# Block transposes and moves in place of PE transposes for 16 of 26 context chunks in a cross-attention kernel

## The chip, the core and the metric

The kernel runs on one core of a Trainium2 chip, and the metric is the time of one execution on the device in microseconds. The core has a matrix engine (PE, which multiplies and accumulates into PSUM), a vector engine (DVE), a scalar engine (ACT), GpSimd (POOL) and a sync engine (SP), which here only issues transfers. ACT issues transfers too. PE's weight loads are listed apart as PEld. All data are 32-bit floats.

## The reference, cut to what matters

The computation is a cross-attention layer followed by a small recurrence. Only the first lines bear on the change: the context `ctx_1024` (3202 keys of 512 features) is layer-normalised and projected to keys and values for 8 heads of 64.

```python
x = _layernorm(builder_state, g1, beta1)          # 4096 x 512 queries
base_n = _layernorm(base_state, g1, beta1)        # 3202 x 512 context
x = residual + _mha(x, base_n, W_qkv, b_qkv, W_o, b_o)
# inside _mha, per head:
#   k = base_n @ Wk.T + bk ; v = base_n @ Wv.T + bv
#   attn = softmax(q k^T / 8) ; out = attn @ v
xn = _layernorm(x, g2, beta2)
U = (xn @ W_in.T + b_in) @ Bmat
# s_t = silu(s_{t-1} @ A.T) + u_t, over all t
x = residual + states @ Cmat + mod
```

Softmax and the weighted sum over keys do not depend on the order of the keys, as long as keys and values have the same order.

## The kernel before, in words

The program has two large stages. The first, the preparation, turns the context into keys and values and stores them in device memory; it takes the first 216 us. The second, attention, goes through 64 units (blocks of 512 queries by pairs of heads, in halves), with a planner that orders its pieces by costs and due times; the recurrence and the output rows run beside it. The change touches the preparation alone. Its instructions are in a fixed order, written out by hand (`manual_schedule`): each engine and each transfer queue runs its own instructions in the order of the program text.

The context is worked in 26 chunks of 128 keys (the last has 2), in groups of `GC = 4`. For chunk c:

- `load_chunk` (L544) loads it from device memory into `cx`, on SP's queue, five chunks ahead in program order.
- `norm_chunk` makes its statistics on DVE (L259, L261), three small operations on POOL (L268, L270, L272) and the normalised rows `xh` on ACT (L280). The loop does this for chunk c+3.
- `turn_chunk`, for chunk c+2, transposes `xh` in four 128x128 blocks on PE (L296, tile `tp_c`) and copies the result from PSUM into the group's tile `ct`, on ACT for even chunks and on DVE for odd ones (L575). `ct` holds features on the partitions and keys along the row; two such tiles alternate.
- The values: eight matmul instructions with `ct` as the stationary operand (L623, tile `pv`), a copy to `vs` on ACT (L636) and a store `vd` on SP (L637).
- At the end of a group the keys: for each of the four head pairs (`hp`) eight matmul instructions with `ct` as the moving operand (L656, tile `pk`), the bias on ACT into `ks` (L664) and two stores `kd` on SP (L669). `pv` and `pk` have two PSUM tiles each.

Between these, a generator called `side` is advanced by one step at a time (`next(work)`, once per chunk and once or twice per head pair). It holds work on the weights and constants (loads on ACT's queue of `win`, `cb`, `rowb`, `modb`, `wp_t`, `a_t`, `wo`; small products such as `pw`, `pt`, `pb`; the sum `sums` over `cb`, L509, and its product `pm`, L515) and then the first queries: four tiles are normalised, transposed on PE (`tp_x`, L296) and copied, and three head pairs of queries are made (`pq`, L325).

The functions `flip` and `move` are already used in attention, for query rows and output rows: `flip` transposes 32x32 blocks of one chunk by one DVE instruction (L1057) into half of the columns of a pair of chunks, and `move` carries one band of 32 partitions of that pair to its place in the transposed tile by four transfers within SBUF of 32 KB each (L1069). Four moves serve one pair; each gives 64 columns, in which 32 come from one chunk and 32 from the other.

Of the kernel before, what the change touches and what calls it, by code (L numbers as in the profile page):

```python
# [10 lines left out]
F32 = mybir.dt.float32  # L11
# [8 lines left out]
T, S2, H, NH, HD, NS = 4096, 3202, 512, 8, 64, 64  # L20
P = 128
TB = 32
NC = H // P
NCH = 26
CK = 128
NDC = NCH // 2
REST = S2 - (NCH - 1) * CK
GC = 4
# [3 lines left out]
QU = QB // 2  # L32
LAG = 4
FIRST = 3
EPS = 1e-5
L = 16
LT = 4
# [16 lines left out]
def keys(c):  # L54


    return CK if c < NCH - 1 else REST


def blocks(c):  # L60

    return 2 if c < NDC - 1 else 1


def key0(c):
    return c * CK
# [117 lines left out]
def xattn_ssm_kernel(  # L184
# [22 lines left out]
    nc = tc.nc  # L207
# [56 lines left out]
    def factors(mv, n, name, pool=None):  # L264

        pool = pool or ln
        ve = pool.tile([P, 1], F32, tag="ve", name=f"ve_{name}")
        nc.gpsimd.tensor_scalar(ve[:n], mv[:n, 1:2], EPS, None, ALU.add)  # L268
        rstd = pool.tile([P, 1], F32, tag="rstd", name=f"rstd_{name}")
# [71 lines left out]
    def first_queries(x0):  # L341

        xn = first_xn["xn"] = xnp.tile([P, NC, QB], F32, tag="xn", name="xn_0")
        for t in range(NT):
# [10 lines left out]
            yield  # L355
        for hp in range(FIRST):
            pieces = heads(0, hp, xn)
# [34 lines left out]
    wp = prep.enter_context(tc.tile_pool(name="wkv", bufs=1))  # L392
    cin = prep.enter_context(tc.tile_pool(name="cin", bufs=3))
    ctp = prep.enter_context(tc.tile_pool(name="cT", bufs=2))
# [140 lines left out]

    cxs, xhs, cts = {}, {}, {}

    def load_chunk(c):  # L540
        if c < NCH:
# [5 lines left out]
    def norm_chunk(c):  # L547
        if c < NCH:
            xhs[c] = normalize(cxs.pop(c), keys(c), f"c{c}", pool=cin)


    def first_chunk(c):
        xt, name = cxs.pop(c), f"c{c}"
        mv = stats(xt, P, name, cin)
        ve = cin.tile([P, 1], F32, tag="ve", name=f"ve_{name}")
        nc.vector.tensor_scalar(ve, mv[:, 1:2], EPS, None, ALU.add)
        rstd = cin.tile([P, 1], F32, tag="rstd", name=f"rstd_{name}")
# [8 lines left out]
    def turn_chunk(c):  # L566
        if c < NCH:
            g, n = c // GC, keys(c)
            if c % GC == 0:
                cts[g] = ctp.tile([P, NC, GC * CK], F32, tag="ct", name=f"ct_{g}")  # L570
            o = key0(c) - key0(g * GC)
            copy = nc.vector.tensor_copy if c % 2 else nc.scalar.copy
            tp = transposes(kps, "t", xhs.pop(c), n, f"c{c}")
            for cs in (slice(0, 2), slice(2, NC)) if c == 0 else (slice(0, NC),):
                copy(cts[g][:, cs, o : o + n], tp[:, cs])  # L575

    with tc.manual_schedule():
        load_chunk(0)
        nc.scalar.dma_start(g1s, g1)
        fetch_w(2, nc.scalar, slice(0, NC // 2))  # L580
        fetch_w(2, nc.sync, slice(NC // 2, NC))
        load_chunk(1)
        load_chunk(2)
        fetch_w(1, nc.sync)
        load_chunk(3)
        idle = m_tile([P, 512], "idle")
        nc.scalar.copy(bu, neg_half)
        for _ in range(11):
            nc.tensor.matmul(idle[:, :P], a_t, a_t, start=True, stop=True)
        for t, src in ((be1s, beta1), (bqkv, b_qkv), (g2s, g2), (be2s, beta2)):  # L590
            nc.sync.dma_start(t, src)
        for c in range(4, 5):
            load_chunk(c)
        early = [first_chunk(c) for c in range(2)]
        next(early[0])
        next(early[0])
        turn_chunk(0)
        gain(2, wv, 0)
        gain(2, wv, 1)
        next(early[1])  # L600
        gain(2, wv, 2)
        norm_chunk(2)
        gain(2, wv, 3)
        next(early[1])
        work = side()
        first = shift(1)
        loads = [partial(load_k, *steps[k]) for k in range(AHEAD_K - 1)]
        loads += [partial(load_v, *steps[k]) for k in range(AHEAD - 1)]
        for c in range(NCH):
            load_chunk(c + 5)  # L610
            if c >= 2 * AHEAD_K:
                for _ in range(4):
                    if loads:
                        loads.pop(0)()
            norm_chunk(c + 3)
            g, n = c // GC, keys(c)
            ct, o = cts[g], key0(c) - key0(g * GC)
            pv = kps.tile([P, 512], F32, tag="v", name=f"pv_{c}")
            parts = 1 if c < NCH - 1 else 2
            for i in range(NC // parts):  # L620
                for h in range(parts):
                    k = h * NC // parts + i
                    nc.tensor.matmul(  # L623
                        pv[h * HD : h * HD + n, :H],
                        ct[:, k, o : o + n],
                        wv[:, k, :],
                        start=(i == 0),
                        stop=(i == NC // parts - 1),
                        skip_group_check=True,
                    )  # L630
            if c == 0:
                turn_chunk(1)
            turn_chunk(c + 2)
            if c < NCH - 1:
                vs = cin.tile([CK, NC, P], F32, tag="vs", name=f"vs_{c}")
                nc.scalar.copy(vs, pv)  # L636
                nc.sync.dma_start(vd[:, c // 2, :, c % 2, :].rearrange("h p d -> p h d"), vs)  # L637
            else:
                second = wp.tile([n, H], F32, name="second")
                nc.scalar.copy(second, pv[HD : HD + n])  # L640
                nc.vector.tensor_tensor(vx[:n], pv[:n], second, ALU.add)
                nc.sync.dma_start(vx[HD : HD + n], vx[:n])
            if c < GC:
                if c == 1:
                    gain(1, wk)
                for _ in range((0, 0, 1, 2)[c]):
                    next(first)
            else:
                next(work, None)
            if c % GC < GC - 1 and c < NCH - 1:  # L650
                continue
            n_g = o + n
            for hp in range(NC):
                pk = kps.tile([P, 512], F32, tag="k", name=f"pk_{g}_{hp}")
                for i in range(NC):
                    nc.tensor.matmul(  # L656
                        pk[:, :n_g],
                        wk[:, i, hp * P : (hp + 1) * P],
                        ct[:, i, :n_g],
                        start=(i == 0),  # L660
                        stop=(i == NC - 1),
                    )
                ks = cin.tile([P, GC * CK], F32, tag="ks", name=f"ks_{g}_{hp}")
                nc.scalar.activation(  # L664
                    ks[:, :n_g], pk[:, :n_g], AF.Identity, bias=bias[:, NC + hp : NC + hp + 1]
                )
                for b in range(g * GC, c + 1, 2):
                    m, k = blocks(b // 2) * CK, key0(b) - key0(g * GC)
                    nc.sync.dma_start(kd[hp, b // 2, :, :m], ks[:, k : k + m])  # L669
                if g == 0:  # L670
                    nc.gpsimd.tensor_copy(kx[:, hp, REST:], ks[:, : HD - REST])
                elif c == NCH - 1:
                    nc.gpsimd.tensor_copy(kx[:, hp, :REST], ks[:, CK : CK + REST])
                for _ in range(2 if g > 1 else 1):
                    next(work, None)
        left = sum(1 for _ in work)
        assert left == 0, left
# [315 lines left out]
    def queries(plan, Q, d):  # L993
# [55 lines left out]
                    copied.append((*ks[t], "copy"))  # L1049
            d += 2 * QSTEP  # L1050
        head_pieces(plan, Q, range(NC), w, copied, d, QSTEP // 2, [("xn", of_xn)])

    def flip(pair, xh, t):

        nc.vector.transpose(  # L1057
            pair.rearrange("p t h -> p (t h)").rearrange("p (g t r) -> p t g r", t=2, r=TB)[:, t],
            xh.rearrange("p (g r) -> p g r", r=TB),
        )  # L1060

    def move(xn, pair, a):

        n = 2 * TB
        of = pair[a * TB : (a + 1) * TB].rearrange("p t h -> p (t h)").rearrange(
            "p (c b k) -> p b c k", b=P // TB, k=n
        )
        for b in range(P // TB):
            nc.sync.dma_start(xn[b * TB : (b + 1) * TB, :, a * n : (a + 1) * n], of[:, b])  # L1069

    def mixed(of, t):
        return of.rearrange("p (a t r) -> p t a r", t=2, r=TB)[:, t]
# [507 lines left out]
    def unit(plan, i):  # L1580
# [16 lines left out]
        w["shift"] = shifts[:, Q * NC + hp : Q * NC + hp + 1]  # L1597
        q = [("q", Q, hp)] if Q or hp >= FIRST else []
        first = i if half == 0 else index[Q, hp, 0]
# [281 lines left out]
    with tc.manual_schedule():  # L1881
# [5 lines left out]
                xn=1, xh=2, max=2, rd=2, o_=12,  # L1887
            ),
            dict(q=[("heads", 0, hp) for hp in range(FIRST)], xn=["first"]),
        )  # L1890
        head_pieces(plan, 0, range(FIRST, NC), first_xn, [("spread", 0)], -40 * STEP, 0, [("xn", "first")], "o")
        index = {at_: i for i, at_ in enumerate(units)}
# [12 lines left out]
    n = nc.values_load(sv["nbad"][0:1, 0:1], min_val=0, max_val=P * (NCK + P // LT + 3 * len(units)))  # L1905
    with tc.If(n > 0, label="general"):
# [14 lines left out]
        with tc.For_i(0, 2 * P // LT, 1):  # L1921
            sl, th, h = sv["sl"], sv["thl"], sv["hw"][:, : P // LT]
# [71 lines left out]
```

## Time and profile before

| | |
|---|---|
| runs | 1963.19, 1963.2, 1960.02 us; median 1963.19 |
| profiled execution | 1960.71 us, span 1958.9, mean granted clock 0.996 |
| PE busy | 98% of the span |
| DVE, ACT, POOL busy | 74%, 60%, 12% |
| preparation | from 0 to about 216 us |
| context transposes on PE | 104 instructions, the first at 6.1, the last at 192.7 us |
| key stretches (L656) | from 25.7, 56.7, 91.0, 122.8, 152.9, 192.8 and 212.0 us |

In a timeline row the first two numbers are the start and the length in us, then the engine (with q: its instruction queue, as for issues of transfers), the line, the operation, and the output tile with its inputs; brackets hold the idle time of the engine before it and what ended that. In a group row the last numbers are the count, then busy us and mean ns. In a wait row they are the total, the number of times and the longest. In a row on transfers they are the count, the KB of each and the median us from issue to landing.

### The profile page before, as it was taken

The numbers are of one execution on the slowest core, as the hardware profiler recorded it, in microseconds if no ns is written. First come the engines' busy times: TensorE is split into PE (matmuls) and PEld (weight loads), VectorE is DVE, ScalarE is ACT, GpSimd is POOL, SyncE is SP. The second block draws the span as 40 slices with busy tenths as digits, with TensorE's granted clock in tenths as the row PEclk, the third lists the DMA queues.
The fourth block names the chain that finished last, engine by engine and source line by source line (L and its number), as shares of the span: only waits on it lengthen the run. The fifth ranks groups of instructions, "written<-read, shape, count | busy, mean of one in ns | idle before, by whom it ended". The sixth has DMA issues, their size and how long they took to land. (4 is left out here: it accounts for less than half of the span.)

```text
span 1958.9 us, 66935 instructions
## 1 busy us (share of the span) xinstructions
PE 1928.9 (98%) x29092; PEld 1259.3 (64%) x29092; DVE 1459.3 (74%) x1983; ACT 1171.3 (60%) x1632; POOL 225.5 (12%) x374
## 2 busy tenths in 40 slices
PE   9999999999999999999999999999999999999996
PEld 5444577666667666666667666666666666766674
DVE  4321489688878887888868886888778886877876
ACT  2233477566666666666657665666666675665653
POOL 2111000001200120011100120012001100011105
PEclk9999999999999999999999999999999999999998
DMA  6533234123422243223312342224322331544476
GB/s 195 172 102 108 64 85 115 48 86 88 129 79 80 86 114 84 74 83 109 104 47 86 92 121 77 81 87 122 87 82 75 95 96 43 156 134 141 143 207 199
DMA packets 246935, 204.28 MB, mean 104 GB/s; under 512 B 80809, under 2 KB 220073, under 8 KB 246637
## 3 DMA queue, kind: packets, MB, share of 16 engines
q1 hardware_dynamic: 242616, 193.32, 34.1%
q10 hardware_dynamic: 4020, 6.62, 1.1%
q8 instruction: 231, 3.78, 0.8%
q14 instruction: 68, 0.55, 0.1%
HBM read 156.32 MB, written 29.88 MB: 95 GB/s over the span
## 5 line engine op out<-in xcount | busy, mean ns | idle before, releaser
L783 ACT ACTIVATE p<-s,shifts 128x1024 f32<-128x1024 f32 (+1 forms) x832 | 890.1, 1081 | 482.9 <-PE s L706 474.3
L791 DVE TENSOR_TENSOR acc<-p,acc 128x1024 f32<-128x1024 f32 (+1 forms) x704 | 830.5, 1180 | 203.6 <-ACT p L783 169.8
L840 PE MATMUL po<-p,v 64*64 64x256 f32 x12800 | 834.1, 377 | 2.7 <-DVE o L889 2.5
L706 PE MATMUL s<-q,k 64*64 64x256 f32 x12800 | 834.9, 377 | 1.8 <-ACT p L783 1.8
L706 PEld LDWEIGHTS s<-q,k 64*64 64x64 f32 x12800 | 490.4, 133 | 214.2 <-issue 13.3
L840 PEld LDWEIGHTS po<-p,v 64*64 64x64 f32 x12800 | 485.0, 133 | 192.6 <-issue 12.0
L1110 POOL TENSOR_TENSOR xr<-xr,rowb 128x512 f32<-128x512 f32 x30 | 42.7, 1436 | 984.9 <-DMA xr<-in_x_dram 984.9
L912 DVE RECIPROCAL rd<-rd 128x256 f32<-128x256 f32 (+1 forms) x64 | 110.2, 1722 | 13.0 <-ACT rd L907 12.7
L325 PE MATMUL pq<-xn,wq 128*128 128x512 f32 x248 | 110.7, 598 | 0.0
L1116 PE MATMUL pa<-wo,o 128*128 128x512 f32 x240 | 107.0, 599 | 0.0
L623 PE MATMUL pv<-wv,ct 128*128 128x512 f32 (+1 forms) x208 | 92.6, 595 | 0.9 <-DVE wv L406 0.9
L656 PE MATMUL pk<-ct,wk 128*128 128x512 f32 (+1 forms) x224 | 88.9, 550 | 0.0
L575 DVE COPY ct<-tp_c 128x512 f32<-128x512 f32 (+1 forms) x13 | 8.4, 649 | 105.7 <-PE tp_c L296 105.7
L791 DVE TENSOR_TENSOR acc<-p,p 128x1024 f32<-128x1024 f32 x64 | 78.1, 1221 | 10.6 <-ACT p L783 10.6
L325 PEld LDWEIGHTS pq<-xn,wq 128*128 128x128 f32 x248 | 45.7, 190 | 55.5 <-issue 54.3
L1116 PEld LDWEIGHTS pa<-wo,o 128*128 128x128 f32 x240 | 44.4, 190 | 56.0 <-issue 55.5
L815 DVE TENSOR_TENSOR acc<-swap,acc 64x256 f32<-64x256 f32 x126 | 60.5, 480 | 11.1 <-ACT swap L810 9.4
L656 PEld LDWEIGHTS pk<-ct,wk 128*128 128x128 f32 x224 | 39.2, 190 | 42.6 <-issue 42.6
L623 PEld LDWEIGHTS pv<-wv,ct 128*128 128x128 f32 (+1 forms) x208 | 36.8, 186 | 43.4 <-issue 41.1
L664 ACT ACTIVATE ks<-pk,bias 128x512 f32<-128x512 f32 (+1 forms) x28 | 18.0, 642 | 74.7 <-PE pk L656 67.6
L810 ACT COPY swap<-acc 64x256 f32<-64x256 f32 x126 | 50.9, 404 | 16.9 <-DVE acc L798 14.4
L334 ACT ACTIVATE q<-pq,bias 128x512 f32<-128x512 f32 x31 | 21.3, 688 | 62.5 <-PE pq L325 62.5
(222 smaller groups left out, 1217.9 us busy)
## 6 DMA issues: line engine op xcount, KB each, us to landing
k<-kd SPq DMA_DIRECT2D x432, 128.0 KB, 2.3
v<-vd SPq DMA_DIRECT2D x432, 128.0 KB, 2.1
xn<-x SPq DMA_DIRECT2D x416, 32.0 KB, 1.9
xr<-in_x_dram SPq DMA_DIRECT2D x30, 256.0 KB, 3.5
x1d<-xr SPq DMA_DIRECT2D x30, 256.0 KB, 2.2
x<-in_x_dram SPq DMA_DIRECT2D x28, 256.0 KB, 3.2
cx<-in_ctx_dram SPq DMA_DIRECT2D x25, 256.0 KB, 3.3
vd<-vs SPq DMA_DIRECT2D x25, 256.0 KB, 2.4
```

Of the source, the lines that this page charges most:

```text
L325: nc.tensor.matmul(pq, wq[:, i, hp * P : (hp + 1) * P], xn[:, i, :], start=(i == 0), stop=(i == NC - 1),)
L623: nc.tensor.matmul(pv[h * HD : h * HD + n, :H], ct[:, k, o : o + n], wv[:, k, :], start=(i == 0), stop=(i == NC // parts - 1), skip_group_ ...
L656: nc.tensor.matmul(pk[:, :n_g], wk[:, i, hp * P : (hp + 1) * P], ct[:, i, :n_g], start=(i == 0), stop=(i == NC - 1),)
L706: nc.tensor.matmul(s[k0 : k0 + HD, a, b, :], kts[(*w["at"][:2], c)][r, b * CK + k0 : b * CK + k0 + HD], q[r], start=True, stop=True, skip_ ...
L783: nc.scalar.activation(t[:, :, :nb, :], w["ps"][c][:, :, :nb, :], AF.Exp, bias=w["shift"])
L791: nc.vector.tensor_tensor(w["acc"][:, :, :nb, :], t[:, :, :nb, :], before[:, :, :nb, :], ALU.add)
L810: nc.scalar.copy(w["swap"][r], of[(1 - k) * HD : (2 - k) * HD])
L815: nc.vector.tensor_tensor(of[r], w["swap"][r], of[r], ALU.add)
L840: nc.tensor.matmul(w["po"][a * HD : (a + 1) * HD, k, :QU], vts[Q, hp, c][r, b, a * HD : (a + 1) * HD], t[r, a, b, :], start=(c == 0 and b ...
L912: nc.vector.reciprocal(w["rd"][:, part], (w["pd"] if last else w["rd"])[:, part])
L1110: nc.gpsimd.tensor_tensor(v["x"], v["x"], rowb, ALU.add)
L1116: nc.tensor.matmul(v["pa"], o_t[Q, c, half][:, t * P : (t + 1) * P], wo[:, c, :], start=(c == 0), stop=(c == NC - 1),)
```

## The change

For chunks 8 to 23, groups 2 to 5, the transposes on PE and the copies from PSUM are replaced. The two chunks of a pair are flipped by two DVE instructions into a tile `pair`, which takes the place in SBUF of weight tiles that are no longer needed, and four moves of four transfers each carry the pair into `ct`: parts 0 and 1 on SP's queue, parts 2 and 3 on ACT's. So 16 chunks lose 64 transposes on PE, 8 copies on ACT and 8 on DVE, and gain 16 flips and 128 transfers. The keys of a pair then lie in a mixed order, the same for keys and values.

The places in the program order are these. Two chunks are normalised together at odd c (c+3 and c+4). The first pair of a group is flipped where its first chunk was transposed, two chunks before the group begins; its parts 0 and 2 are issued at the start of the last chunk of the group before, its parts 1 and 3 behind head pair 0 of that group's key matmuls. The second pair is flipped behind head pair 1, with its parts 0 and 2 there, and parts 1 and 3 behind head pair 2. `flip` and `move` stand earlier in the text and are otherwise as before; `move` gains the queue as an argument.

```diff
+FLIPS = 2
...
+    def flip(pair, xh, t):
+        nc.vector.transpose(
+            pair.rearrange("p t h -> p (t h)").rearrange("p (g t r) -> p t g r", t=2, r=TB)[:, t],
+            xh.rearrange("p (g r) -> p g r", r=TB),
+        )
+    def move(xn, pair, a, queue=nc.sync):
+        n = 2 * TB
+        of = pair[a * TB : (a + 1) * TB].rearrange("p t h -> p (t h)").rearrange(
+            "p (c b k) -> p b c k", b=P // TB, k=n
+        )
+        for b in range(P // TB):
+            queue.dma_start(xn[b * TB : (b + 1) * TB, :, a * n : (a + 1) * n], of[:, b])
...
+    def flip_pair(c):
+        g, k = divmod(c, GC)
+        if k == 0:
+            pairs[g] = wp.tile([P, NC, H], F32, tag="raw_" + "vqkq"[g - FLIPS], name=f"pair_{g}")
+        for t in range(2):
+            flip(pairs[g][:, k : k + 2], xhs.pop(c + t), t)
+
+    def move_pair(c, a):
+        g, k = divmod(c, GC)
+        if k == a == 0:
+            cts[g] = ctp.tile([P, NC, GC * CK], F32, tag="ct", name=f"ct_{g}")
+        for part, queue in ((a, nc.sync), (2 + a, nc.scalar)):
+            move(cts[g][:, :, k * CK : (k + 2) * CK], pairs[g][:, k : k + 2], part, queue)
+
+    def flips(c):
+        return FLIPS * GC <= c < NCH // GC * GC
...
-            norm_chunk(c + 3)
+            if not flips(c + 3):
+                norm_chunk(c + 3)
+            if flips(c + 3) and c % 2:
+                norm_chunk(c + 3)
+                norm_chunk(c + 4)
+            if flips(c + 1) and c % GC == GC - 1:
+                move_pair(c + 1, 0)
...
-            turn_chunk(c + 2)
+            if not flips(c + 2):
+                turn_chunk(c + 2)
+            elif (c + 2) % GC == 0:
+                flip_pair(c + 2)
...
+                if hp == 0 and flips(c + 1):
+                    move_pair(c + 1, 1)
+                if hp in (1, 2) and flips(c + 3):
+                    if hp == 1:
+                        flip_pair(c + 3)
+                    move_pair(c + 3, hp - 1)
                 for _ in range(2 if g > 1 else 1):
                     next(work, None)
```

More of the change, by code (lines that the diff above doesn't have):

```diff
@@ L534, in side @@
         yield from first_queries(x0)
-    cxs, xhs, cts = {}, {}, {}
+    def flip(pair, xh, t):
[10 more added lines that the diff above has]
+            queue.dma_start(xn[b * TB : (b + 1) * TB, :, a * n : (a + 1) * n], of[:, b])
+    cxs, xhs, cts, pairs = {}, {}, {}, {}
     def load_chunk(c):
@@ L1051, in queries @@
         head_pieces(plan, Q, range(NC), w, copied, d, QSTEP // 2, [("xn", of_xn)])
[L1055 to L1069, printed above, removed]
     def mixed(of, t):
```

## The prediction

> **What bounds the kernel now.** I read the page's head first, then the stretches that the change touches, cut at the matmuls that begin them.
>
> ```profile
> span 1958.9 us, 66935 instructions
> PE 1928.9 (98%) x29092; PEld 1259.3 (64%) x29092; DVE 1459.3 (74%) x1983; ACT 1171.3 (60%) x1632; POOL 225.5 (12%) x374
> ...
> 52.87:73.44 20.57, 20.57 (x62) 9.29 (x61) 4.17 (x12) 4.66 (x8) 1.44 (x5) 1.00 0.67 202
> 73.44:106.86 33.42, 33.22 (x105) 15.75 (x104) 12.70 (x25) 8.77 (x14) 6.42 (x19) 1.00 0.41 127
> 106.86:136.96 30.10, 30.10 (x89) 14.55 (x88) 5.99 (x14) 11.37 (x18) 6.30 (x18) 1.00 0.36 105
> 136.96:167.06 30.10, 30.10 (x89) 14.55 (x88) 5.22 (x12) 10.89 (x17) 5.25 (x15) 1.00 0.35 105
> ```
>
> Each stretch row gives length, then PE, PEld, DVE, ACT, POOL, clock, DMA share, GB/s. PE is busy throughout at clock 1.00; ACT and DVE are under 40% busy. PE runs its instructions in order, so a matmul taken away is a gain, and any operand that comes late is a loss that nothing later gives back. I call the value matmuls of chunk c V(c), the key matmuls of one head pair K, the transposes of a chunk T(c).
>
> **What is saved.** The timeline of PE around chunks 10 and 11, and the transposes of chunks 8 to 23 as a group:
>
> ```profile
> 81.96 0.60 PE L296 MATMUL tp_c<-ident,xh_c 128*128 128x128 f32 x4
> 82.40 3.60 PE L623 MATMUL pv<-wv,ct 128*128 128x512 f32 x8
> 85.83 0.60 PE L296 MATMUL tp_c<-ident,xh_c 128*128 128x128 f32 x4
> 86.64 0.28 PE L515 MATMUL pm<-ones,sums 128*64 128x1 f32 x2 [0.20 <-DVE sums L509]
> ...
> L296 PE MATMUL tp_c<-ident,xh_c x64: 272/273/273, 52.4 to 178.1; 128*128 128x128 f32 x64
> ```
>
> From the start of T to the start of V(10) is 82.40-81.96 = 0.44 us; V itself takes 85.83-82.40 = 3.43, and a K the same. Sixteen T go: 16 x 0.44 = **7.0 us**. The 0.4 us that pm loses to sums today (85.83+0.44 to 86.64) is counted again below, so 7.4 stand against the new waits. On transposes the row of 273 ns is a length, not a pace. [...]
>
> The removed copies (8 on DVE, 8 on ACT) and the 16 added block transposes lie on engines with room; their rows, those of the transfers, and the price of a move:
>
> ```profile
> L1057 DVE STREAM_TRANSPOSE x<-xh_x x24: 668/704/712, 280.2 to 1380.8; 128x512 f32<-128x512 f32 x24
> ...
> L1069 SPq DMA_DIRECT2D xn<-x x416: 585/599/1953, 283.9 to 1803.9; - x139
> ...
> DMA to landing us min/median/max: 1.9/1.9/4.9
> ```
>
> A flip is 0.70 on DVE (idle over 60%): zero, if xh is there. A part is four transfers; at 0.60 each plus the gap 0.65, so 2.6 us of the issuing queue, landing 1.9 after the last issue. Sixteen transfers per pair, half on SP, half on **ACT's own instruction stream**: 64 x 0.65 = 42 us of ACT. No move on ACT is in the trace; I take SP's row, since other issues cost ACT as much as SP. Below, 0.4 (those rows), above 1.95.
>
> Further edits, each with one answer. Keys of a pair change places alike in K and V, so their matmuls keep shape and length: zero. kd, vd and the loads of the last chunks keep their places on SP; eight moves per pair come between them, 5.2 us of SP in a stretch of 27 or more, so what is late there is late by the waits below, not by the issues. The flips of the second pair stand on DVE ahead of a head pair's side work, 1.4 us in idle time. Normalising two chunks at every odd c puts the second a chunk sooner on DVE, POOL and ACT, while its load keeps its place on SP: it has one chunk's time less cover. What stands behind it is sums on DVE and vs on ACT; place 1 prices this.
>
> **The wait that the code does not show.** SP's issues at the start, its waits, and landings:
>
> ```profile
> 2.75 0.44 SPq L402 DMA_DIRECT2D raw_k<-in_L_xattn_W_qkv_dram  x1
> ...
> 7.88 0.90 SPq L544 DMA_DIRECT2D cx<-in_ctx_dram  x2
> ```
> ```profile
> SPq L591 <- DMA raw_v<-in_L_xattn_W_qkv_dram: 2.3, 1, 2.3
> SPq L637 <- DMA raw_k<-in_L_xattn_W_qkv_dram: 1.9, 1, 1.9
> ```
> ```profile
> cx<-in_ctx_dram SPq DMA_DIRECT2D x25, 256.0 KB, 3.3
> ...
> kd<-ks SPq DMA_DIRECT2D x48, 128.0 KB, 1.8
> ...
> raw_k<-in_L_xattn_W_qkv_dram SPq DMA_DIRECT2D x1, 1024.0 KB, 7.9
> raw_q<-in_L_xattn_W_qkv_dram ACTq DMA_DIRECT2D x1, 1024.0 KB, 5.9
> ...
> wo<-in_L_xattn_W_o_dram ACTq DMA_DIRECT2D x1, 1024.0 KB, 7.8
> ...
> cb<-in_ctxb_2048x_dram ACTq DMA_DIRECT2D x1, 800.0 KB, 5.1
> ...
> a_t<-in_L_xattn_A_dram ACTq DMA_DIRECT2D x2, 16.0 KB, 5.5
> ```
>
> The store of chunk 0's values (L637) has nothing to do with raw_k, yet waits for it: SP is free at 8.78, raw_k lands at 2.75+7.9 = 10.65, the wait is 1.9. In program order raw_k is the 7th transfer, this store the 15th; g2s (L591), the 11th, waits for raw_v, whose ACT half is the 3rd. So **a transfer waits until the one eight before it, on either queue, has landed**. In a head pair with moves the order is kd, kd, four on SP, four on ACT: ACT's last move waits for that head pair's own second kd, so ACT is held from the end of ks for 0.4 (first kd issued) + 1.8 (second lands) + 0.6 (last issue) = 2.8, and the next ks comes 0.7+2.9 = 3.6 us after this one, against PE's 3.43. That small lag has a cover: key PSUM tiles are two deep. Two places have less.
>
> [...]
>
> **Place 1, chunks 7 to 11.** ACT, PE, SP and DVE there, before:
>
> ```profile
> 53.08 0.35 ACTq L453 DMA_DIRECT2D cb<-in_ctxb_2048x_dram  x1
> ...
> 56.55 0.58 ACT L636 COPY vs<-pv 128x512 f32<-128x512 f32 x1 [1.61 <-PE pv L623]
> ...
> 58.21 1.31 ACTq L466 DMA_DIRECT2D a_t<-in_L_xattn_A_dram  x2
> 60.38 0.69 ACT L664 ACTIVATE ks<-pk,bias 128x512 f32<-128x512 f32 x1 [3.24 <-PE pk L656]
> ```
> ```profile
> 69.95 3.65 PE L656 MATMUL pk<-ct,wk 128*128 128x512 f32 x8
> 73.44 3.60 PE L623 MATMUL pv<-wv,ct 128*128 128x512 f32 x8
> ...
> 78.42 3.70 PE L623 MATMUL pv<-wv,ct 128*128 128x512 f32 x8
> ```
> ```profile
> 75.29 0.40 SPq L544 DMA_DIRECT2D cx<-in_ctx_dram  x1
> ```
> ```profile
> 83.68 2.91 DVE L509 TENSOR_REDUCE sums<-cb 128x64 f32<-128x1600 f32 x1
> 86.50 0.69 DVE L259 BATCH_NORM_STATS2 st_c<-cx 128x6 f32<-128x512 f32 x1
> ```
> ```profile
> 88.82 0.81 ACT L280 ACTIVATE xh_c<-cx,nmr_c,rstd_c 128x512 f32<-128x512 f32 x1 [6.08 <-POOL nmr_c L272]
> ```
>
> After: cb lands near 58; ACT's first moves (pair 8, part 2) wait for it and end at 59.6, so vs(7) and the five loads behind it slip 3 us, the a_t issues to about 61.6 and ks of the first head pair to 62.4. Part 3's moves wait for those a_t, +5.5 = 67.3, end 69.3; wo, which today comes right behind the first ks, follows at 69.3, then ks of head pair 1 (held from 64.6), 70.4: the fourth K, due at 69.1 (69.95 less two T), needs the PSUM tile that this ks empties and starts at 70.5, **1.4 late**. The second move behind that is eight after wo: held until wo lands, 69.3 + 6.9 (between raw_q's 5.9 and wo's 7.8) = 76.2; three more issues, ks of head pair 2 at 78.2, its two kd, then SP's moves of pair 10 part 1, landing 83.8. On PE the fourth K ends at 73.9, V(8) with the side work behind it takes 78.42-73.44-0.44 = 4.5, V(9) ends at 81.9, so V(10), which needs part 1, waits **1.9**. ks of head pair 3 comes at 82.5; SP issues the load of chunk 13 only behind its kd, 84.2 against 75.29, landing 87.5. Chunk 13's statistics are now normed a chunk earlier, which puts them ahead of sums on DVE: 0.9 for them, then 3.4 to the end of sums (0.5 of small copies), 91.8. pm is in PE's order behind V(10), which ended at 87.2: **4.6**. Place 1 costs 7.9. Bounds: 0 if ACT is not held, 10.5 with slower landings throughout.
>
> **Place 2, the query tiles' transposes in key stretches.**
>
> ```profile
> 122.79 7.03 PE L656 MATMUL pk<-ct,wk 128*128 128x512 f32 x16
> 129.66 0.60 PE L296 MATMUL tp_x<-ident,xh_x 128*128 128x128 f32 x4
> ...
> 126.42 0.69 ACT L664 ACTIVATE ks<-pk,bias 128x512 f32<-128x512 f32 x1 [3.24 <-PE pk L656]
> 127.01 0.80 ACT L280 ACTIVATE xh_x<-x,nmr_x,rstd_x 128x512 f32<-128x512 f32 x1
> ```
>
> tp_x needs xh_x, which ACT now runs behind the moves: 0.1+0.7+2.8+0.8 = 4.4 after the end of the K before, and PE is there after 3.43: 1.0 late if ACT is on time. It is not: chunk 17's load follows the kd of the stretch before, its xh gates vs(13), vd(13) gates chunk 19's load, that its xh, and vs(15) and the first ks follow. Counted from the end of the former K: load 3.6, landing 6.9, xh 10.0 (86.50 to 89.63 is 3.1), vs 10.6, load 11.1, landing 14.4, xh 17.4, moves and vs to 20; PE needs 4 x 3.43 + 0.44 + 3.43 = 17.6 to the end of the first K. Late by 2.1 to 2.4, so **3.0** here. In chunk 19's stretch the same, one head pair later, with most of the lag gone after this wait: between 1.1 and 3.4, taken at **1.7**.
>
> **Sum.** -7.4 + 7.9 + 3.0 + 1.7 = +5.2 us, taken as +5. Attention behind it is PE-bound and only shifts. The traced execution took 1960.71 (span 1958.9), the runs' median is 1963.19: 1965.7 or 1968.2, so I say **1967**; its own range is 1962 to 1973.
>
> **Rivals.**
> - *Faster, 1954 to 1956.* ACT's queued transfers do not hold its activations, or the eight-apart wait spares moves. Then ACT's 2.6 us per part fit beside 3.43 and only -7.4 remains. For it: ACT is under 40% busy. Against: SP's waits. It decides if wo lands by 68, where sums meet V(10) without a wait; it is issued only then. 0.2.
> - *No change, 1960 to 1963.* Constants land in 4 instead of 5.5 and ACT is on time in both key stretches: 5.4 + 1.0 + 1.1 against 7.4. 0.2.
> - *Much slower, about 1976.* Moves and kd on two queues land later: at 3.9 (two thirds of the way from 1.9 to the moves' longest, 4.9) a head pair's cycle is 0.7+0.4+3.9+0.6+0.1 = 5.7, 2.3 over PE's; three in a row make 6.9, 3.4 more than the PSUM cover of one K, in each of four stretches 13.6, in place of place 2's 4.7: -7.4+7.9+13.6 = +14. Against: DMA share 0.35 to 0.41 leaves room, except 0.67 in the first stretch. 0.12.
>
> The forecast keeps 0.48. A half of the first and most of the third are left out of 1955 to 1975. A change within 0.2% (3.9 us) is about what a measurement of this kernel cannot tell from none: same 0.2 (mostly the second rival), slower 0.56, faster 0.24.
>
> **What would show it.** V(8) to V(12): gaps on PE before V(10) (released by a move) and before pm (by sums), wo issued near 69, chunk 13's load near 84. tp_x in chunks 15 and 19 waiting for xh_x. ACT idle between ks and moves, released by transfers. If instead V(8) starts 0.9 before 73.44 and PE never waits for a move, the faster rival holds; if PE waits at every fourth K, the third. Wrong also if ACT's issues are far from 0.65.

## The result

The changed kernel takes 1967.12 us (median of 13 runs) against 1961.89 for the kernel before (13 runs beside it on the same chip): a ratio of 1.0028, 95% interval 1.0019 to 1.0036, so 5.2 us slower. The profiled execution took 1967.2 us with a span of 1965.4, 6.5 more than that of the kernel before.

The head of the page and the four stretches that were shown of before, cut at the same times:

```profile
span 1965.4 us, 66944 instructions
PE 1926.2 (98%) x29028; PEld 1254.5 (64%) x29028; DVE 1466.5 (75%) x1991; ACT 1168.5 (59%) x1624; POOL 224.7 (11%) x374
...
52.87:73.44 20.57, 17.52 (x41) 6.83 (x40) 3.43 (x8) 4.01 (x6) 2.10 (x6) 0.92 0.63 174
73.44:106.86 33.42, 29.60 (x90) 13.35 (x89) 13.85 (x30) 7.24 (x12) 5.15 (x12) 1.00 0.61 168
106.86:136.96 30.10, 27.71 (x68) 11.96 (x66) 9.27 (x21) 9.12 (x14) 7.84 (x23) 1.00 0.56 141
136.96:167.06 30.10, 27.49 (x67) 12.61 (x67) 6.75 (x14) 10.07 (x16) 5.83 (x17) 0.94 0.53 137
```

64 matmuls are gone, but PE, which had no gap in these stretches, now has gaps in each (3.0, 3.8, 2.4 and 2.6 us), and its granted clock is below 1 in the first and the last. The timeline of PE shows where the gaps lie:

```profile
61.44 3.70 PE L703 MATMUL pk<-ct,wk 128*128 128x512 f32 x8
68.18 5.40 PE L703 MATMUL pk<-ct,wk 128*128 128x512 f32 x8 [3.05 <-ACT ks L711]
...
74.25 3.65 PE L703 MATMUL pk<-ct,wk 128*128 128x512 f32 x8
78.77 3.67 PE L667 MATMUL pv<-wv,ct 128*128 128x512 f32 x8 [0.86 <-DMA ct<-pair]
...
83.39 7.13 PE L667 MATMUL pv<-wv,ct 128*128 128x512 f32 x16
93.40 0.25 PE L516 MATMUL pm<-ones,sums 128*64 128x1 f32 x2 [2.88 <-DVE sums L510]
...
126.81 3.70 PE L667 MATMUL pv<-wv,ct 128*128 128x512 f32 x8 [2.39 <-ACT vs L683]
...
139.99 1.12 PE L297 MATMUL tp_x<-ident,xh_x 128*128 128x128 f32 x4 [2.61 <-ACT xh_x L281]
140.90 8.26 PE L703 MATMUL pk<-ct,wk 128*128 128x512 f32 x16
...
174.03 0.66 PE L297 MATMUL tp_x<-ident,xh_x 128*128 128x128 f32 x4 [0.40 <-ACT xh_x L281]
...
216.70 5.41 PE L667 MATMUL pv<-wv,ct 128*128 128x512 f32 x16
```

The last of these rows is V(24), where the changed part is over. It began at 206.68 before, so the preparation is 10.0 us longer, not 5. Two things behind it make that smaller. Up to the last computed value attention took 0.7 us less in this execution, and the closing branch of the program, which chooses between the normal end and a general path, took PE's sequencer 4 us less. Of before, and then of after:

```profile
1952.31 0.14 DVE L1741 CAST nbad<-py 1x1 int32<-1x1 f32 x1
...
L1906 PEldq COMPARE_BRANCH  x1: 4455/4455/4455, 1953.4 to 1953.4; - x1
```
```profile
L1776 DVE CAST nbad<-py x1: 136/136/136, 1961.6 to 1961.6; 1x1 int32<-1x1 f32 x1
...
L1941 PEldq COMPARE_BRANCH  x1: 405/405/405, 1962.7 to 1962.7; - x1
```

From the last value to the end of the span, before took 1958.9-1952.3 = 6.6 us and after 1965.4-1961.6 = 3.8. So 10.0-0.7-2.8 = 6.5 us.

ACT and DVE in place 1, and the waits that grew most (window 40 to 225; total, times, longest):

```profile
61.38 0.81 ACT L281 ACTIVATE xh_c<-cx,nmr_c,rstd_c 128x512 f32<-128x512 f32 x1 [5.64 <-POOL nmr_c L273]
61.44 2.70 ACTq L555 DMA_DIRECT2D ct<-pair  x4
...
67.44 0.69 ACT L711 ACTIVATE ks<-pk,bias 128x512 f32<-128x512 f32 x1 [2.67 <-DMA rowb<-in_L_xattn_b_o_dram]
67.46 4.70 ACTq L555 DMA_DIRECT2D ct<-pair  x4
72.20 0.60 ACTq L469 DMA_DIRECT2D wo<-in_L_xattn_W_o_dram  x1
72.86 0.69 ACT L711 ACTIVATE ks<-pk,bias 128x512 f32<-128x512 f32 x1 [4.73 <-DMA ct<-pair]
72.94 6.25 ACTq L555 DMA_DIRECT2D ct<-pair  x4
79.23 0.69 ACT L711 ACTIVATE ks<-pk,bias 128x512 f32<-128x512 f32 x1 [5.69 <-DMA ct<-pair]
```
```profile
59.05 0.69 DVE L260 BATCH_NORM_STATS2 st_c<-cx 128x6 f32<-128x512 f32 x1 [5.48 <-DMA cx<-in_ctx_dram]
...
89.06 0.69 DVE L260 BATCH_NORM_STATS2 st_c<-cx 128x6 f32<-128x512 f32 x1 [12.51 <-DMA cx<-in_ctx_dram]
```
```profile
DVE st_c L260 <- DMA cx<-in_ctx_dram: 82.2, 9, 17.9
...
ACT ks L711 <- DMA ct<-pair: 27.6, 8, 5.7
```

The reader is to see a chain. Chunk 11's statistics wait for its load until 59.05, its `xh` therefore comes on ACT at 61.38, and only behind it stand the moves of part 2, `vs`, five constants, and ks of the first head pair at 67.44. The third K needs the PSUM tile that this ks empties, and begins at 68.18. Further down, chunk 13's load keeps DVE from `sums`, and `pm` from PE.

The first link is no late issue: chunk 11's load went out at 52.93, and in the run with no moves (below) at 52.50, where its statistics began at 56.03. It landed some 3 us later here, with SP's first moves (from 54.63) in flight beside it; whether these delayed it is not shown.

### The profile page after: what moved, and what is told of

It is laid out like the page before. It is cut to its first block, busy times and chain, and to the rows that moved or that the text cites. A ratio compares the mean times of both kernels' runs of the same rounds, so it can differ in the third digit from the quotient of the medians.

```text
span 1965.4 us, 66944 instructions
## 1 busy us (share of the span) xinstructions
PE 1926.2 (98%) x29028; PEld 1254.5 (64%) x29028; DVE 1466.5 (75%) x1991; ACT 1168.5 (59%) x1624; POOL 224.7 (11%) x374
## 4 chain that ended last, share of the span: by engine, by line
## 5 line engine op out<-in xcount | busy, mean ns | idle before, releaser
L260 DVE BATCH_NORM_STATS2 st_c<-cx 128x6 f32<-128x512 f32 (+1 forms) x26 | 17.7, 679 | 85.1 <-DMA cx<-in_ctx_dram 85.1
L830 DVE TENSOR_TENSOR acc<-x,acc 2x256 f32<-2x256 f32 x128 | 53.0, 414 | 2.4
```

What stands on the lines that cost most here:

```text
L830: nc.vector.tensor_tensor(to[r], t[r], to[r], ALU.add)
```

## The experiments

Two theories stood at first. (A): the loads are late, because normalising in pairs took away a chunk of cover. (B): ACT is held by the moves that it issues itself. Each experiment was judged by the time, by the start of V(24) and by the end. V(24) is the better gauge of the preparation: from its start to the last value the profiled executions differ by up to 6.9 us (1743.7 to 1750.6), with attention's code the same in all.

| run | us, and before beside it | ratio (95%) | V(24), to before | end behind last value |
|---|---|---|---|---|
| changed kernel | 1967.12, 1961.89 | 1.0028 (1.0019 to 1.0036) | 216.70, +10.0 | 3.8 |
| no moves | 1953.91, 1961.99 | 0.9963 (0.9950 to 0.9975) | 199.51, -7.2 | 3.8 |
| norms in pairs only | 1962.05, 1960.43 | 1.0005 (0.9994 to 1.0016) | 206.82, +0.1 | 6.4 |
| loads earlier | 1955.75, 1961.99 | 0.9970 (0.9959 to 0.9982) | 204.66, -2.0 | 3.8 |
| before, loads earlier | 1963.36, 1959.57 | 1.0010 (0.9999 to 1.0021) | 206.83, +0.1 | 6.7 |
| wo at chunk 8 | 1966.86, 1961.99 | 1.0025 (1.0014 to 1.0036) | 211.51, +4.8 | 3.8 |
| GpSimd for ACT | 1963.97, 1961.99 | 1.0020 (1.0010 to 1.0029) | 206.00, -0.7 | 10.3 |
| all moves on SP | 1985.94, 1960.43 | 1.0116 (1.0100 to 1.0133) | 231.37, +24.7 | 3.8 |
| loads earlier, wo at chunk 8 | 1956.31, 1960.43 | 0.9978 (0.9965 to 0.9990) | 203.83, -2.9 | 3.8 |
| loads earlier, GpSimd | 1957.53, 1960.43 | 0.9984 (0.9973 to 0.9994) | 200.12, -6.6 | 10.2 |
| loads earlier, wo behind pm | 1959.21, 1959.57 | 0.9996 (0.9981 to 1.0011) | 207.80, +1.1 | 3.8 |
| loads earlier, wo and x0 exchanged | 1953.83, 1961.73 | 0.9965 (0.9952 to 0.9979) | 200.77, -5.9 | 3.8 |
| more idle matmuls (2 runs) | 1977.11, 1959.57 | 1.0082 (1.0057 to 1.0107) | 222.42, +15.7 | 3.8 |

**No moves: what the transposes are worth.** The moves are left out and `ct` is filled with a constant, so that the keys and values of 16 chunks are not computed; the rest of the program runs as it is.

```diff
+            nc.gpsimd.memset(cts[g], 0.01)
...
-            move(cts[g][:, :, k * CK : (k + 2) * CK], pairs[g][:, k : k + 2], part, queue)
+            pass
```

> Leaves out all 64 moves on SP and the 64 on ACT: the chunks of groups 2 to 5 are filled with a constant by GpSimd, so keys and values of 16 chunks are wrong; the block transposes and the paired normalising stay. It shows what the missing transposes are worth without the price of moving, and what the paired normalising costs by itself. If all loss is in the moves (B): no new wait on PE, -7.0 from the transposes, so 6 to 8 us less than the kernel before. If the paired normalising makes the loads late by itself (A): waits of pm and of V(15) stay, 2 to 5 us of them, so 2 to 5 us less than the kernel before.

V(24) begins 206.68-199.51 = 7.2 us earlier: the 7.0 of the transposes and pm's old 0.2. PE waits for nothing that the change brought. Yet the statistics still wait 64.6 us for their loads, against 82.2 in the changed kernel:

```profile
199.51 5.41 PE L668 MATMUL pv<-wv,ct 128*128 128x512 f32 x16
```
```profile
DVE st_c L260 <- DMA cx<-in_ctx_dram: 64.6, 10, 15.7
```

So (A) alone is not it: a load may be late and cost nothing, as long as no move stands behind what waits for it. The same is seen from the other side.

**Norms in pairs only, in the kernel before.**

```diff
+    def flips(c):
+        return 2 * GC <= c < NCH // GC * GC
...
-            norm_chunk(c + 3)
+            if not flips(c + 3):
+                norm_chunk(c + 3)
+            if flips(c + 3) and c % 2:
+                norm_chunk(c + 3)
+                norm_chunk(c + 4)
```

> The kernel before, with the paired normalising of chunks 8 to 23 alone: no block transposes, no moves, all transposes stay on TensorE. (A) If a chunk of cover less for the odd loads costs by itself: statistics wait for cx, and pm or a V waits, 2 to 5 us more than the kernel before. (C) If the loads are late only in a loop with the moves (a move holds ks, ks holds kd, kd holds the next load on SP, the load holds the next normalising, and that holds ACT ahead of the next move), as the run without moves suggests: no new wait on PE, within 2 us of the kernel before.

V(24) at 206.82 and a ratio of 1.0005: no cost, although the statistics wait 49.4 us for loads. This fits (C), a loop of loads and moves, and not (A).

**Loads one chunk earlier.**

```diff
-        for c in range(4, 5):
+        for c in range(4, 6):
             load_chunk(c)
...
-            load_chunk(c + 5)
+            load_chunk(c + 6)
```

> Every context chunk's load stands one chunk further ahead in SP's order; nothing else is changed. Two theories of the 16 us of new waits on PE. (A) Late loads: normalising in pairs took one chunk of cover from the odd chunks' loads, and the loads of chunks 11, 13 and 17 land behind it. Then the statistics stop waiting for cx (17.9 us in 9 waits now), ACT's second part of moves in place 1 is no longer held by the normalising of chunk 11, and three waits of PE go or shrink: key matmuls of the third head pair 3.3 and their slow clock 1.8, pm 3.1, V(15) 2.55. 7 to 10 us less than the changed kernel, which is 2 to 5 us less than the kernel before. (B) ACT held by its own moves and by wo: the loads are late only because ks is late; a load that stands further ahead spares V(15)'s 2.55 at most and leaves the third head pair and pm, so 2 to 5 us more than the kernel before.

V(24) begins 12.0 us earlier than in the changed kernel. The kernel is 6.2 us faster than the one before; 2.0 of that are the preparation and 2.8 the end, and the rest no single profile can place. The waits of the third K, V(15) and pm are gone or small, and the K and the V behind the two waits left in place 1 have rows of 3.70 and 3.67. PE and ACT in this run:

```profile
61.51 7.45 PE L703 MATMUL pk<-ct,wk 128*128 128x512 f32 x16
...
70.44 3.70 PE L703 MATMUL pk<-ct,wk 128*128 128x512 f32 x8 [0.64 <-ACT ks L711]
75.80 3.67 PE L667 MATMUL pv<-wv,ct 128*128 128x512 f32 x8 [1.66 <-DMA ct<-pair]
...
87.49 0.28 PE L516 MATMUL pm<-ones,sums 128*64 128x1 f32 x2
```
```profile
64.52 0.69 ACT L711 ACTIVATE ks<-pk,bias 128x512 f32<-128x512 f32 x1 [2.80 <-DMA rowb<-in_L_xattn_b_o_dram]
...
69.04 0.61 ACTq L469 DMA_DIRECT2D wo<-in_L_xattn_W_o_dram  x1
69.69 0.69 ACT L711 ACTIVATE ks<-pk,bias 128x512 f32<-128x512 f32 x1 [4.49 <-DMA ct<-pair]
69.78 6.44 ACTq L555 DMA_DIRECT2D ct<-pair  x4
76.26 0.69 ACT L711 ACTIVATE ks<-pk,bias 128x512 f32<-128x512 f32 x1 [5.88 <-DMA ct<-pair]
```

A control shows that the earlier loads gain nothing by themselves: the same edit in the kernel before.

> A control: the kernel before with every context chunk's load one chunk further ahead, and nothing of the change. If the early loads gain only because they cut the loop of moves and loads, there is nothing to gain here but pm's 0.4 us: within 2 us of the kernel before. If they gain by themselves, 4 to 6 us less than the kernel before, and the change would have no part in the gain of the run with early loads.

V(24) at 206.83 against 206.68, ratio 1.0010. So the 12 us are a cost that loads and moves have only together, in a loop: a move holds ks, ks holds kd, kd holds the next load on SP, that load holds the next normalising, and this holds ACT ahead of the next moves. That the moves make a load late can be read from SP's issue of chunk 13's load, in the changed kernel and then with no moves:

```profile
85.79 0.45 SPq L563 DMA_DIRECT2D cx<-in_ctx_dram  x1
```
```profile
74.54 0.40 SPq L563 DMA_DIRECT2D cx<-in_ctx_dram  x1
```

With the norms in pairs only it goes out at 75.44. An earlier load opens the loop at one place.

**GpSimd for ACT's half: the loop opened at another place.**

```diff
-        for part, queue in ((a, nc.sync), (2 + a, nc.scalar)):
+        for part, queue in ((a, nc.sync), (2 + a, nc.gpsimd)):
```

> The half of the moves that ACT issues is issued by GpSimd instead; nothing else is changed. (B) ACT is then not held by 2.6 us of issues per part: ks, vs and xh_x come on time, tp_x in chunk 15's key stretch does not wait (2.8 now) and the third head pair of place 1 waits less than 3.3; 4 to 7 us less than the changed kernel, so between 2 us less and 1 us more than the kernel before. (A) The waits that come from late loads stay (5 to 8 us of 16), and only tp_x's 2.8 go. A third possibility: GpSimd, which also makes the small factor of each normalising (nmr_c), is held by the moves in its turn and xh comes late: then as slow as the changed kernel or slower.

V(24) is 10.7 us earlier than in the changed kernel, tp_x waits nowhere, and the third K doesn't wait; V(8) (1.31) and pm (2.65) do. The loads are still late (75.0 us of waits of the statistics). So freeing ACT does nearly as much as freeing the loads, which fits a loop. The time does not follow: 2.0 us more than before. The end of the program is 6.5 us longer than in the changed kernel (10.3 against 3.8), and most of that is a drain of GpSimd's queue:

```profile
L2025 POOLq DRAIN  x3: 40/103/5304, 1953.8 to 1959.7; - x3
```

In the changed kernel the longest of the three takes 78 ns. It is long in both runs in which GpSimd issued moves and in no other.

**All moves on SP.**

```diff
-        for part, queue in ((a, nc.sync), (2 + a, nc.scalar)):
+        for part, queue in ((a, nc.sync), (2 + a, nc.sync)):
```

> All moves of a pair are issued by SyncE, none by ACT; nothing else is changed. If what costs is that ACT is held (2.6 us of issues per part, and waits for landings behind constants and wo), this comes out like the kernel with that half on GpSimd: prep 10 us less than in the changed kernel, 0 to 3 us more than the kernel before. If what costs is that the chunk loads go out late (they stand on SP behind kd and moves), SP's further 2.6 us per part put them later still: as slow as the changed kernel or slower, 5 to 9 us more than the kernel before.

25.5 us more than before: the second case of the expectation in kind, at three times its size. SP issues the chunk loads too, and the statistics now wait 107.3 us for them (82.2 in the changed kernel). The longer gaps of PE that come with it also cost clock (granted 0.70 from 85.8 to 91.0 us and 0.59 from 135.0 to 141.3):

```profile
85.81 5.24 PE L667 MATMUL pv<-wv,ct 128*128 128x512 f32 x8 [4.62 <-DMA ct<-pair]
...
134.99 6.25 PE L667 MATMUL pv<-wv,ct 128*128 128x512 f32 x8 [7.41 <-ACT vs L683]
```

**wo's load, three places.** First, in the changed kernel alone, wo (1 MB) goes behind place 1's key stretch, to the step with the product `pb`:

```diff
-        nc.scalar.dma_start(wo, wo_t.rearrange("(c p) o -> p c o", p=P))
         pw = m_tile([P, 512], "pw")
...
         yield
+        nc.scalar.dma_start(wo, wo_t.rearrange("(c p) o -> p c o", p=P))
         pb = m_tile([P, 512], "pb")
```

> The 1 MB load of wo is moved from between the first and the second head pair of place 1 to chunk 8's side work; nothing else is changed. (B) The moves that stand behind wo on ACT (landing 5.4 to 5.8 us now, 1.9 to 2.1 elsewhere) land in about 2 us, ks of the third head pair comes near 75 instead of 79.2, chunk 13's load goes out near 81 instead of 85.8, V(8) and pm do not wait (1.0 and 3.1 now): 4 us less than the changed kernel, about 1 us more than the kernel before. The 3.3 us before the third K stay, since ks of the first head pair is ahead of wo. (A) The load of chunk 13 is late whatever wo does: pm keeps most of its wait, 0 to 1 us less than the changed kernel.

V(8) doesn't wait, as (B) said, and V(24) is 5.2 us earlier than in the changed kernel; but pm still waits 3.53, as (A) said, and the median is the same (1966.86). Why the median kept nothing of what the profiled execution shows (1962.17 us) stays open; the runs reach from 1961.91 to 1969.89. Then the same with the loads earlier, by the two edits shown:

> Loads one chunk further ahead and wo's load at chunk 8's side work, together. With the loads early, place 1 still costs 3.2 us (0.6 before the fourth K, 1.7 before V(8), 0.9 of slower running before it), all of it behind wo: the two moves parts behind it land 4.5 to 5.9 us after ACT wants to go on. If wo is their cause, those 3 us go: 8 to 9 us less than the kernel before, 2 to 3 less than with the early loads alone. If not (the constants ahead of wo hold ACT as much), the same as with the early loads alone, 5 to 7 us less than the kernel before.

V(24) gains only 0.8 over the earlier loads alone, and the times cannot be told apart: V(8) is on time now, but wo is issued at 77.5, beside the moves of the next pair, and V(10) waits 1.94. Third, with the loads earlier, wo behind pm, away from all moves of place 1:

```diff
-        nc.scalar.dma_start(wo, wo_t.rearrange("(c p) o -> p c o", p=P))
         pw = m_tile([P, 512], "pw")
...
         nc.vector.tensor_scalar(a_t, a_t, 0.5, None, ALU.mult)
+        nc.scalar.dma_start(wo, wo_t.rearrange("(c p) o -> p c o", p=P))
```

> Loads one chunk further ahead, and wo's load issued behind pm, in chunk 10's stretch, where no moves are under way (with wo at chunk 8 V(10) waited 1.9 for moves that were in flight beside it). If wo beside the moves is what is left of place 1's cost, V(8) and V(10) do not wait, and this is 7.5 to 9 us less than the kernel before. If wo, needed for rowv's matmul some 10 us later, now lands too late, that matmul waits instead: 4 to 6 us less, the same as with the early loads alone.

```profile
84.79 0.28 PE L515 MATMUL pm<-ones,sums 128*64 128x1 f32 x2
...
101.95 2.08 PE L531 MATMUL pr<-rowv,ones 128*128 128x512 f32 x2 [4.94 <-DVE rowv L416]
```

pm comes 0.5 later than with no moves at all (84.30): place 1's rest was wo beside moves. But the matmul of rowv, which needs wo, waits 4.94. That is the wait of the expectation's second case, but it costs more than was expected there: the time is the kernel before's, not 4 to 6 us less. Last, with the loads earlier, wo at the place of x0 and x0 behind pm (wo's old line is gone too):

```diff
-        nc.scalar.dma_start(x0, x[:QB, :].rearrange("(t p) h -> p t h", p=P))
+        nc.scalar.dma_start(wo, wo_t.rearrange("(c p) o -> p c o", p=P))
         yield
...
         nc.vector.tensor_scalar(a_t, a_t, 0.5, None, ALU.mult)
+        nc.scalar.dma_start(x0, x[:QB, :].rearrange("(t p) h -> p t h", p=P))
```

> Loads one chunk further ahead, wo's load where that of the first queries (x0, 1 MB too) stands, in chunk 9's stretch, and x0's behind pm, in chunk 10's. In the run with wo behind pm, V(8), V(10) and pm did not wait, but rowv's matmul waited 4.9 for wo, which was issued at 92.6; issued at about 82 it lands near 89, before rowv's matmul needs it at 97. If nothing else is late, the fourth-group values begin 5 to 6 us earlier than in the kernel before, and the time is 7 to 9 us less than that kernel's. If x0, now 10 us later, is late for tp_x in chunk 13's stretch, or holds the moves behind it as wo did, 3 to 6 us less.

It gives 1953.83 us against 1961.73, ratio 0.9965 (0.9952 to 0.9979): faster than both kernels, as the first case of the expectation had it. PE loses 200.77-199.51 = 1.3 us to all moves together.

```profile
96.72 1.02 PE L531 MATMUL pr<-rowv,ones 128*128 128x512 f32 x2
...
200.77 5.41 PE L667 MATMUL pv<-wv,ct 128*128 128x512 f32 x16
```

**Loads earlier and GpSimd**, by the two edits shown.

> Loads one chunk further ahead, and ACT's half of the moves issued by GpSimd. In the run with GpSimd alone V(8) waited 1.3 for a move and pm 2.65 for the sums, which wait for a chunk's statistics, which wait for a late load; with early loads the second goes. Expected if late loads and ACT's hold are separate costs: 7 to 9 us less than the kernel before. If GpSimd's own transfers hold the normalising (it also makes nmr_c): no better than the early loads alone, 4 to 6 us less than the kernel before.

V(24) at 200.12, 0.6 behind the run with no moves: together the two cuts take away nearly all that the moves cost in the preparation. They do not add up, though: against the changed kernel they gain 12.0 and 10.7 us alone and 16.6 together. So the two costs are not separate, as the first case of the expectation had it; much of what one cut gains is what the other would have gained, which again fits a loop. With the end of 10.2 instead of 3.8 the time is 2.9 us below the kernel before, not 9.

**The end of the program.** All kernels with the change end 3.8 us after the last value where GpSimd issues no moves, and the three with before's transposes 6.4 to 6.7. One run asked whether the number of PE's matmuls decides that: it has as many as the kernel before, 29092.

```diff
-        for _ in range(11):
+        for _ in range(43):
             nc.tensor.matmul(idle[:, :P], a_t, a_t, start=True, stop=True)
```

> The changed kernel with 32 more of the idle matmuls at the start, 64 instructions on TensorE, so that its program has as many matmuls as the kernel before. The start gets some 12 us longer and isn't the question; the end is. In the kernel before, TensorE's closing branch took 4.46 us and ended the span 6.6 after the last computed value; in the changed kernel it took 0.41 and 3.8. If the length of TensorE's program decides that, the branch takes 4.5 again and the end is 6.4 to 6.6; if it hangs on something else of the change, 0.4 and 3.8.

The branch took 503 ns, not 4.5 us: the number alone does not decide. What does stays open. The three kernels with the long branch are the three that keep all of before's transposes, but they differ from the others in more than that. The profiles show only that the changed kernel gains 2.8 us there.

## Why the prediction came out right

The time was forecast at +5 and measured at +5.2, in the range and in the direction. The steps were not all as good as that. The run with no moves has no new wait, so its starts on PE are the scale, and each gap of the changed kernel is a difference to it:

| step | forecast, us | measured, us |
|---|---|---|
| transposes saved, with pm's old wait | -7.4 | -7.2 |
| place 1: third K late / slow behind the gap | 0 | 3.2 / 1.8 |
| place 1: fourth K late | 1.4 | 0 |
| place 1: V(8) late | 0 | 1.0 |
| place 1: V(10) late | 1.9 | 0 |
| place 1: pm late | 4.6 | 3.0 |
| V(15) late | 0 | 2.6 |
| tp_x, chunk 15 / slow behind the gap | 3.0 | 2.8 / 1.8 |
| tp_x, chunk 19 | 1.7 | 0.6 |
| rest | 0 | 0.4 |
| sum at V(24) | +5.2 | +10.0 |
| end of the program | 0 | -2.8 |
| attention in the profiled execution | 0 | -0.7 |

- *What is saved.* Right: 0.44 a chunk. The 273 ns of a transpose's row, taken as its pace, would have given 64 x 0.273 = 17.5 us; 7.2 were measured.
- *The price of a move.* Right: four issues on ACT take 2.55 to 2.70 us where nothing disturbs them (2.6 forecast), and the flip 0.70.
- *The eight-apart wait.* Half right. The wait exists: moves on SP waited for transfers that they have nothing to do with, among them wo (3.2 us), x (2.1) and chunk loads (3.9 in three waits). And ACT does stand for its moves, which was an estimate in the forecast: its ks waited 27.6 us for them in 8 waits, and freed of them, V(24) gains 10.7 us. But which transfer holds which was read from the order of the program's text, whereas by the semaphores in the trace, eight of which (100, 102 and 104 to 109) go round among the transfers, SP's and ACT's moves of a pair mostly alternate. "ACT's last move waits for that head pair's own second kd" is not what the trace shows. The hold of 2.8 a part was right in size where nothing else was in flight, since it is nearly the issue time alone; in place 1 the last three of the four parts held ACT for 4.70, 6.25 and 3.54.
- *Place 1.* Forecast 7.9, measured 9.0, but at other places. The walk along ACT gave wo at 69.3, ks of head pair 1 at 70.4 and of head pair 2 at 78.2. The changed kernel had 72.20, 72.86 and 79.23. With the loads earlier, ACT had 69.04, 69.69 and 76.26: the walk was that of a kernel whose loads are in time (where place 1 costs 3.2 us, by pm at 87.49 against 84.30, not 7.9). The step that failed is the sentence on normalising two chunks at once, "What stands behind it is sums on DVE and vs on ACT". The moves and the first ks of the stretch stand behind it too: `xh` of chunk 11 at 61.38 puts ks of the first head pair at 67.44 (62.4 forecast), and the third K waits for that. pm was right in its cause (chunk 13's load issued at 85.8, forecast 84.2; statistics ahead of sums) and 1.6 too long. V(10) did not wait; that the gap before the third K had given its moves the time is likely, but not shown.
- *Place 2.* Right in size and cause for chunk 15 (its own terms, 1.0 and 2.1 to 2.4, add up to 3.1 to 3.4, taken as 3.0). The lag that the forecast followed there, from chunk 17's load over `xh` to vs(13), also empties the PSUM tile of V(15); this was not looked at and cost 2.6. For chunk 19 too much was taken, 1.7 against 0.6; that the wait at chunk 15 had given the loads their time back is likely, but not shown.
- *Not foreseen:* the slower clock behind two of the gaps (granted 0.50 from 69 to 71 and from 140 to 143.3 us), 3.6 together, and the shorter end.

So the number +5 was luck, two errors that cancel: the preparation costs 4.8 us more than forecast, and the end and the execution give 3.5 back in the profile (4.8 in the medians, 10.0 to 5.2, of which 2.8 is the end and 2 no single profile can place). The rival "faster" was right about what could be had: with the loads and wo moved, ACT's issues do fit beside 3.43 us, and the time is 1953.83 (its 1954 to 1956, though 2.8 of that come from the end). The "much slower" rival did not occur; moves land in 2.0 us (median of 53 to 170 us, both queues), in 5.2 to 5.6 beside wo's 1 MB and in 5.5 beside cb's 800 KB.

## What to carry to other kernels

When transfers are put on an engine's queue, list what stands behind each of them and follow that until the chain ends or returns to its start; if it returns, as here from a move over ks, kd and a load back to a move, delays feed each other, and a load issued one step earlier can be worth more than a cheaper move. Before a change with a small loss is dropped, run it once without its cost (here, without the moves): the distance to that ceiling says whether a repair is worth looking for. Compare the moment at which the changed part is over, not only the times: an end of the program that moved by 2.8 us hid more than a quarter of the loss.

## What the runs showed of the hardware

*Clock behind a gap.* Granted clocks of the changed kernel in slices of 10 us, after the gaps before the third K and before tp_x:

```profile
60.00:70.00 10.00, 6.95 (x19) 2.52 (x16) 1.98 (x5) 2.09 (x3) 1.05 (x3) 0.91 0.50 127
70.00:80.00 10.00, 9.14 (x26) 4.33 (x25) 1.95 (x7) 1.38 (x2) 1.05 (x3) 0.92 0.70 188
...
140.00:150.00 10.00, 10.00 (x23) 4.91 (x24) 0.00 (x0) 2.48 (x4) 0.00 (x0) 0.83 0.45 106
```

The gaps that follow are the idle times in the brackets of the rows. The K behind the gap of 3.05 us takes 73.41-68.18 = 5.2 us instead of 3.43; behind one of 2.45 (more idle matmuls) a K has a row of 5.29 instead of 3.60. The longest of these rows are V's, with all moves on SP: 6.42 behind 4.68 and 6.25 behind 7.41. Gaps of 2.39 and less cost no clock in these stretches (the V behind 2.39 has a row of 3.70). In between it varies: the 2.88 before pm cost none (a V of 3.70), while 2.65 at the same place, in the run with GpSimd, was followed by a V of 5.37. What decides between these two is not shown. Behind the gap of 3.05 the granted clock was 0.50 from 69 to 71 us, and the first matmul took 1.17 us, where most take 0.59. Behind those of these gaps that cost clock, a K or V was up to 2.8 us longer (6.42 less 3.60).

*Small transfers beside a large one.* Issues of the changed kernel between 72.5 and 78 us, when wo was in flight, with size and median time to landing:

```profile
wo<-in_L_xattn_W_o_dram ACTq DMA_DIRECT2D x1, 1024.0 KB, 6.2
kd<-ks SPq DMA_DIRECT2D x2, 128.0 KB, 5.4
ct<-pair ACTq DMA_DIRECT2D x3, 32.0 KB, 5.6
ct<-pair SPq DMA_DIRECT2D x2, 32.0 KB, 5.2
```

From 53 to 170 us the moves' median is 2.0 on both queues, and with wo behind pm (loads earlier) those of the same stretch land in 2.1 on both. Beside wo SP's moves landed in 5.2, hardly sooner than ACT's in 5.6, which stand behind wo in its own queue: here the 1 MB load delayed the small transfers of both queues.

*The end.* A closing branch took PE's sequencer 0.4 to 0.5 us in some programs and 4.3 to 4.5 in others, and the two programs whose GpSimd had issued moves drained for 5.3 us at their end. In a kernel where 0.3% is the question, both are to be read off before a time is explained.
